# Keys and values of the third graph layer projected with seven block products in place of eight

## The chip, the cores and the metric

The kernel runs on one core of a Trainium2 chip. The metric is the device time of one execution in microseconds. A core has TensorE (PE: matmuls and transposes; PEld is its weight load), VectorE (DVE), ScalarE (ACT), GpSimd (POOL) and SyncE (SP), which run side by side, each through its own queue in order, and wait for each other through semaphores. Matmul results land in PSUM (eight banks of 512 fp32 values for each of 128 partitions), all else lies in SBUF.

## The reference, cut to what matters

Four graph layers follow each other on 2708 nodes with 512 features; each is `x = layernorm(x + gnn(x, adj))`, and the count starts at 0. The change lies in layer 2:

```python
def _L2_gnn_ref(x, adj, weight, bias, node_w, edge_w):
    node_att = jax.nn.softmax(x @ node_w, axis=0)
    h = x @ edge_w
    e = h @ h.T
    e = jnp.where(adj > 0, e, NEG_BIG)
    edge_att = jax.nn.softmax(e, axis=1)
    combined_att = node_att * edge_att
    support = x @ weight
    output = adj * combined_att @ support
    return output + bias
```

The two projections `x @ edge_w` (the keys) and `x @ weight` (the values) are 2708 x 512 by 512 x 512 products in fp32.

## The kernel before

The nodes are cut into 22 blocks of 128 rows, the last of 20 (`BLOCKS`, `NT = 22`). The 512 features are four chunks of 128 (`C = 4`). Layers 0 and 1 come first; layer 1's last sums are in `xs`, one row block after another. Layer 2 then has a stage of its own (from L1899 on) that makes, for all nodes, the transposed keys `hT` (features on partitions, nodes along), the values `sup` (nodes on partitions, by blocks), the node scores `natt`, and a copy of `x + bias` in memory (`x2_d`). The attention of layer 2 and then layer 3 follow.

In the stage, `PRE` cuts the blocks into seven groups: six of three blocks, and a last one of four (404 columns). For each group:

- `transpose_rows` (L1364) turns each block with four TensorE transposes (L1368) into one PSUM bank, and VectorE copies the bank into `xt_g` (L1369).
- `project_wide` (L1371) makes the keys: for each of four output chunks, four accumulating matmuls (L1376) whose stationary operand is a 128 x 128 piece of `edge_w` (`ew_sb`) and whose moving operand is a chunk of `xt_g`, as wide as the group; ScalarE copies each result to `hT` (L1928).
- For each block, four matmuls (L1934) with the block's piece of `xt_g` as stationary and 512 columns of `weight` (`w2_sb`) as moving operand make its values; ScalarE copies them to `sup` (L1941).
- For each block, VectorE makes the node score (`xn`, L1943) and adds the bias to `xs` (L1953), and GpSimd's queue writes that to `x2_d` (L1954).

In group 1 the layer norms of layer 1's last two blocks (L1915) come in between. After the groups the softmax over `natt` is made, with two reductions over partitions on GpSimd (L1959, L1964).

The matmuls are fp32. Each shows in the profile as two TensorE instructions of the same shape, each with its own weight load, so that 16 matmuls count as 32. A `tc.tile_pool` with `bufs=4` hands out four PSUM banks for each tag: here four for `tp` (transposes and keys) and four for `pr` (values). A bank is handed out again when the last reader of what it held is done.

The instructions of each engine are put in order when the kernel is built. So VectorE's operations for later blocks, whose inputs are ready early, can stand ahead of the copies of an earlier group: in the trace all node scores are made in the first 20 us of the stage.

The attention stage begins with `combine` (L2004): for each pair of value blocks, four VectorE operations (L2009 to L2012) on half rows, some in place in `sup`. What they write besides lies in the memory of `xs`, so the first waits until the writes to `x2_d` have landed. They stand in VectorE's queue before the last groups' values are done. SyncE's queue loads the adjacency (`a_score`, L1423), and `score_products` (L1523) multiplies keys with keys.

Of the kernel before, what the change touches and what calls it, by code (L numbers as in the profile page):

```python
# [8 lines left out]
F32 = mybir.dt.float32  # L9
# [4 lines left out]
ALU = mybir.AluOpType  # L14
# [3 lines left out]
P = 128  # L18
# [11 lines left out]
def gnn_stack_kernel(  # L30
# [83 lines left out]
    def row_stats(y, n):  # L114

        st = small.tile([P, 6], F32, tag="ln_st", name="ln_st")
        nc.vector.bn_stats(st[:n], y)
        mv = small.tile([P, 2], F32, tag="ln_mv", name="ln_mv")
        nc.vector.bn_aggr(mv[:n], st[:n])
        rstd = small.tile([P, 1], F32, tag="ln_rstd", name="ln_rstd")  # L120
        inv_std(rstd[:n], mv[:n, 1:2], LN_EPS)
        return mv[:n, 0:1], rstd[:n]

    def layer_norm(dst, y, n):
        mean, rstd = row_stats(y, n)
        nc.vector.tensor_scalar(dst, y, mean, rstd, ALU.subtract, ALU.mult)
# [62 lines left out]
    with ExitStack() as l0:  # L189
# [31 lines left out]
        def f1_tile(att, odd, name="f1b"):  # L221
            return att.tile([P, HW], F32, tag=f"f1b{odd}", name=name, bufs=HP)
# [513 lines left out]
        with (  # L736
# [4 lines left out]
            psum = first.enter_context(tc.tile_pool(name="ps_p", bufs=1, space=PSUM))  # L741
# [150 lines left out]
            def turn(k, b):  # L892
                return last_turn[0](k, b, k + 1 == HP, [])[0]
# [16 lines left out]
        with (  # L910
# [42 lines left out]
            turned = 0  # L953
            for ci, (c0, w) in enumerate(CHUNKS):
# [3 lines left out]
                for o in range(C):  # L958
# [3 lines left out]
                    ps = pair[:, o % HP, :]  # L962
                    for c in range(C):
# [15 lines left out]
                while turned < NT and sum(BLOCKS[turned]) <= c0 + w:  # L979
                    j0, n = BLOCKS[turned]  # L980
# [246 lines left out]
        xs, w1_sb, x_held = held1["xs"], held1["w1"], held1["x"]  # L1227
# [3 lines left out]
    with (  # L1231
# [12 lines left out]
        work = main.enter_context(tc.tile_pool(name="l1w", bufs=2))  # L1244
        with tc.tile_pool(name="l1a", bufs=1) as pre:
# [3 lines left out]
            turned = 0  # L1249
            for ci, (c0, w) in enumerate(PIECES):  # L1250
# [10 lines left out]
                while turned < NT and sum(BLOCKS[turned]) <= c0 + w:  # L1261
                    it = turned
                    i0, n = BLOCKS[it]
# [30 lines left out]
        for g in range(0, NT, G):  # L1294
            group = range(g, min(g + G, NT))
            c0 = g * P
            w = min(N, c0 + G * P) - c0
            if g == G:
                ew_sb = load_weight(pw2, edge_w, "ew_sb")
                w2_sb = load_weight(pw2, w2, "w2_sb")  # L1300
# [6 lines left out]
            for jt, (j0, m) in enumerate(BLOCKS):  # L1307
                if later and jt % 4 == 3:
                    y, n = later.pop(0)
                    layer_norm(y, y, n)  # L1310
                raw = work.tile([P, G * P], F32, tag="raw", name="raw", bufs=5)
                a = work.tile([P, G * P], F32R, tag="at", name="at", bufs=3)
# [9 lines left out]
                for it in group:  # L1322
                    n = BLOCKS[it][1]
                    at = a[:, (it - g) * P : (it - g) * P + n]
                    for k, half in enumerate(halves):
# [4 lines left out]
                            start=(jt == 0 and k == 0),  # L1330
                            stop=(jt == NT - 1),
                        )
            for it in group:
                n = BLOCKS[it][1]
# [24 lines left out]
    def key_tile(name):  # L1359
        t = featp.tile([P, C, NFULL * P + Q], F32, tag="keys", name=name)  # L1360
        nc.vector.memset(t[:, :, N:], 0.0)
        return t

    def transpose_rows(psum, dst, rows, n, copy):  # L1364

        tp = psum.tile([P, C, P], F32, tag="tp", name="tp")
        for c in range(C):
            nc.tensor.transpose(tp[:, c, :n], rows[:n, c * P : (c + 1) * P], ident[:n, :n])  # L1368
        copy(dst, tp[:, :, :n])  # L1369

    def project_wide(psum, w, xt, width, put):  # L1371

        for o in range(C):
            ps = psum.tile([P, BANK], F32, tag="tp", name="ps_wide")
            for c in range(C):
                nc.tensor.matmul(  # L1376
                    ps[:, :width],
                    w(c, o),
                    xt(c),
                    start=(c == 0),  # L1380
                    stop=(c == C - 1),
                )
            put(o, ps[:, :width])
# [515 lines left out]
    hT = key_tile("hT")  # L1899
    l2_values = ExitStack()  # L1900
    store = l2_values.enter_context(tc.tile_pool(name="store", bufs=1))
    sup = store.tile([P, NT, F], F32, name="sup")
    natt = const.tile([P, NT], F32, name="natt")
    nc.vector.memset(natt, -3.0e38)
    with (
        tc.tile_pool(name="l2w", bufs=2) as work,
        tc.tile_pool(name="l2ps", bufs=4, space=PSUM) as psum,
    ):
        PRE = [list(range(g, min(g + 3, NT))) for g in range(0, NT - 1, 3)]
        if NT % 3 == 1:  # L1910
            PRE[-1].append(NT - 1)
        PW = sum(BLOCKS[it][1] for it in PRE[-1])
        for gi, group in enumerate(PRE):
            for y, n in last_rows if gi == 1 else ():
                layer_norm(y, y, n)  # L1915
            c0, w = group[0] * P, sum(BLOCKS[it][1] for it in group)
            xt = work.tile([P, C, max(PW, 3 * P)], F32, tag="xt", name="xt_g")
            for b, it in enumerate(group):
                n = BLOCKS[it][1]
                transpose_rows(  # L1920
                    psum, xt[:, :, b * P : b * P + n], xs[:, it, :], n, nc.vector.tensor_copy
                )
            project_wide(
                psum,
                lambda c, o: ew_sb[:, c, o * P : (o + 1) * P],
                lambda c: xt[:, c, :w],
                w,
                lambda o, ps: nc.scalar.copy(hT[:, o, c0 : c0 + w], ps),  # L1928
            )
            for b, it in enumerate(group):  # L1930
                i0, n = BLOCKS[it]
                ps = psum.tile([P, F], F32, tag="pr", name="ps_sup")
                for c in range(C):
                    nc.tensor.matmul(  # L1934
                        ps[:n],
                        xt[:, c, b * P : b * P + n],
                        w2_sb[:, c, :],
                        start=(c == 0),
                        stop=(c == C - 1),
                    )  # L1940
                nc.scalar.copy(sup[:n, it, :], ps[:n])  # L1941
                xn = work.tile([P, F], F32, tag="xn", name="xn")
                nc.vector.scalar_tensor_tensor(  # L1943
                    xn[:n],
                    xs[:n, it, :],
                    1.0,
                    nw_sb[:n],
                    ALU.mult,
                    ALU.mult,
                    accum_out=natt[:n, it : it + 1],  # L1950
                )

                nc.vector.tensor_tensor(xs[:n, it, :], xs[:n, it, :], b2_sb[:n], ALU.add)  # L1953
                nc.gpsimd.dma_start(x2_d[i0 : i0 + n], xs[:n, it, :])  # L1954
# [21 lines left out]
    with (  # L1976
# [8 lines left out]
        held = rows_tile("held").rearrange("p t f -> p (t f)")  # L1985
# [192 lines left out]
        for t in range(start3 + steps + LAG):  # L2178
# [98 lines left out]
```

## Time and profile before

| what | value |
|---|---|
| median of three runs | 3120.9 us (3119.28 to 3121.2) |
| profiled execution, its time | 3120.7 us |
| profiled execution, its span | 3118.8 us |
| TensorE busy | 3070.6 us, 98% |
| VectorE busy | 2025.3 us, 65% |
| ScalarE busy | 1353.1 us, 43% |
| stage of the change, from its first transpose to its last L1934 pass | 1393.6 to 1553.0 us |
| L1934 (values), 176 TensorE instructions, mean | 596 ns |
| L1376 (keys), 224 TensorE instructions, mean | 489 ns |
| granted TensorE clock, mean of the execution | 0.997 |

The span runs from the first to the last instruction of the core; the time of the execution has a little around it. The duration of one instruction reaches past the start of the next, since both are pipelined: the mean of 596 ns for a 512-wide pass is more than the distance from one such pass to the next. To see what a pass takes, read the start of the first and of the one after the last, and divide by their number. In the chain of waits each piece is the time from one start to the next, so its pieces can be divided directly.

### The profile page before, as it was taken

How to read it: one execution, taken by the hardware profiler on the slowest of the kernel's cores; microseconds unless marked ns; L12 is line 12 of the kernel's file. 1: busy time of each engine (PE TensorE's matmuls, PEld its weight loads, DVE VectorE, ACT ScalarE, POOL GpSimd, SP SyncE). 2: the span in 40 equal slices, each digit the busy share in tenths (PEclk: the TensorE clock that was granted, in tenths of full speed). 3: DMA queues.
4: the chain of work that ended last, by engine and by line, in shares of the span. 5: the costliest groups of instructions: out<-in, count | busy, mean ns of one | idle time of the engine just before them, and what ended most of it. 6: DMA issues, size and time to landing. Idle time of an engine off the chain costs nothing.

```text
span 3118.8 us, 39610 instructions
## 1 busy us (share of the span) xinstructions
PE 3070.6 (98%) x15144; PEld 2336.9 (75%) x15144; DVE 2025.3 (65%) x3804; ACT 1353.1 (43%) x1655; POOL 175.2 (6%) x301
## 2 busy tenths in 40 slices
PE   8999999999999999999999999999999999999999
PEld 7999996544444447875588887787778888888886
DVE  7988966785885783452366668677555555555565
ACT  7999998587767350001133334435211111111111
POOL 1111100000000000000111101000010000000000
PEclk9999999999999999999999999999999999999999
DMA  8987964266445315530254445566331111111110
GB/s 277 333 313 251 321 235 144 79 232 221 161 173 192 108 42 158 144 97 31 67 166 133 136 138 165 164 177 184 108 95 36 50 51 51 51 51 50 50 52 29
DMA packets 207228, 430.10 MB, mean 138 GB/s; under 512 B 22218, under 2 KB 137598, under 8 KB 201294
## 3 DMA queue, kind: packets, MB, share of 16 engines
q1 hardware_dynamic: 182774, 326.20, 34.0%
q0 software_dynamic: 24256, 101.35, 8.9%
q8 instruction: 119, 1.95, 0.3%
q14 instruction: 71, 0.58, 0.1%
q10 hardware_dynamic: 8, 0.02, 0.0%
HBM read 330.07 MB, written 95.87 MB: 137 GB/s over the span
## 4 chain that ended last, share of the span: by engine, by line
PE 79%; ACT 8%; DVE 8%; issue 3%; DMA 1%; SPq 0%; DVEq 0%; ACTq 0%; POOLq 0%
PE po L1728 21%; PE ps_s L1523 18%; PE po L650 9%; PE ps_nb L1326 7%; PE ps_wide L1376 5%; PE po L548 4%; ACT t L383 4%; ACT t L515 3%; DVE t L378 2%; PE ps_v L131 2%; PE ps_sup L1934 2%; PE ps_hid L131 2%; PE ps_dec L1093 2%; PE ps_mlp L964 1%; DVE a L444 1%
## 5 line engine op out<-in xcount | busy, mean ns | idle before, releaser
L378 DVE SCALAR_TENSOR_TENSOR t<-t,a 128x2708 f32<-128x2708 f32 (+1 forms) x152 | 443.8, 2922 | 166.1 <-ACT t L383 165.8
L548 PE MATMUL po<-xw,t 128*128 128x129 f32 (+2 forms) x3872 | 428.2, 277 | 11.8 <-DVE rc L781 4.9
L548 PEld LDWEIGHTS po<-xw,t 128*128 128x128 f32 (+2 forms) x3872 | 422.8, 189 | 16.4 <-issue 7.9
L383 ACT ACTIVATE t<-f1b,f2h 128x1354 f32<-128x1354 f32 x296 | 404.4, 1412 | 34.2 <-PE po L650 34.2
L1523 PE MATMUL ps_s<-q,hT 128*128 128x256 f32 (+1 forms) x1848 | 405.5, 372 | 0.0
L1728 PE MATMUL po<-sup,e 128*128 128x256 f32 (+1 forms) x1512 | 398.2, 384 | 5.6 <-DVE c L1809 2.8
L650 PE MATMUL po<-t,emb 128*128 128x452 f32 (+3 forms) x1056 | 399.1, 547 | 4.3 <-ACT t L635 4.2
L1523 PEld LDWEIGHTS ps_s<-q,hT 128*128 128x128 f32 x1848 | 339.5, 190 | 49.5 <-issue 5.1
L650 PEld LDWEIGHTS po<-t,emb 128*128 128x128 f32 (+1 forms) x1056 | 194.2, 191 | 202.1 <-issue 189.2
L1728 PEld LDWEIGHTS po<-sup,e 128*128 128x128 f32 (+1 forms) x1512 | 264.7, 185 | 59.6 <-issue 19.8
L1728 PE MATMUL po<-held,T 128*128 128x256 f32 x1200 | 293.8, 380 | 0.0
L1728 PEld LDWEIGHTS po<-held,T 128*128 128x128 f32 x1200 | 227.0, 190 | 31.1 <-issue 0.9
L2129 DVE SCALAR_TENSOR_TENSOR e<-a_cols,ps_s 128x512 f32<-128x512 f32 (+1 forms) x121 | 79.6, 658 | 233.8 <-PE ps_s L1523 229.9
L1523 PE MATMUL ps_s<-hT 128*128 128x256 f32 (+2 forms) x968 | 213.8, 372 | 0.8 <-ACT sup L1941 0.7
L515 ACT ACTIVATE t<-t 128x2708 f32<-128x2708 f32 x88 | 209.2, 2377 | 8.8 <-DVE t L378 8.1
L1523 PEld LDWEIGHTS ps_s<-hT 128*128 128x128 f32 x968 | 175.1, 190 | 29.1 <-issue 3.9
L1326 PE MATMUL ps_nb<-hid_hi,at 128*128 128x512 f32 x484 | 185.6, 390 | 0.4 <-DVE at L1318 0.4
L635 ACT ACTIVATE t<-t 128x2708 f32<-128x2708 f32 x64 | 157.3, 2458 | 60.4 <-DVE t L378 60.2
L1326 PE MATMUL ps_nb<-hid_lo,at 128*128 128x512 f32 x462 | 180.0, 390 | 0.0
L2031 ACT ACTIVATE a_score<-a_score,neg_big 128x512 f32<-128x512 f32 (+3 forms) x131 | 88.4, 683 | 196.0 <-DMA a_score<-in_adjT_dram 98.9
L2121 ACT ACTIVATE q<-ps_wide,uq 128x256 f32<-128x256 f32 (+1 forms) x44 | 20.5, 465 | 335.7 <-PE ps_wide L1376 335.7
L1633 ACT ACTIVATE e<-e 128x512 f32<-128x512 f32 (+1 forms) x187 | 113.8, 615 | 118.2 <-DVE e L1632 117.9
(276 smaller groups left out, 3995.4 us busy)
## 6 DMA issues: line engine op xcount, KB each, us to landing
a<-adj_d SPq DMA_DIRECT2D x113, 677.0 KB
a_cols<-in_adjT_dram SPq DMA_DIRECT2D x200, 256.0 KB
kept<-t POOLq DMA_DIRECT2D x20, 1354.0 KB, 8.4
t<-kept SPq DMA_DIRECT2D x20, 1354.0 KB
raw<-in_adjT_dram SPq DMA_DIRECT2D x105, 256.0 KB
a<-in_adjT_dram SPq DMA_DIRECT2D x37, 677.0 KB
adj_d<-a POOLq DMA_DIRECT2D x37, 677.0 KB, 6.2
a_score<-in_adjT_dram SPq DMA_DIRECT2D x55, 256.0 KB
```

The lines of the kernel that those rows point to most:

```text
L131: nc.tensor.matmul(ps[:n], xt[:, c, :n], w[:, c, :], start=(c == 0), stop=(c == C - 1))
L378: return nc.vector.scalar_tensor_tensor(t, t, GUARD, ab, ALU.add, ALU.mult)
L383: done = nc.scalar.activation(t[:, k, :], f1b[k][:n, :w], AF.Tanh, bias=f2h[:n, jt, h : h + 1], scale=0.5,)
L515: nc.scalar.activation(t, t, AF.Exp, scale=0.5)
L548: nc.tensor.matmul(po[k][b][:m, s * DR : (s + 1) * DR], t[own : own + n, k, i0 : i0 + m], values[own : own + n, jt, HP * p + k, :], start= ...
L635: nc.scalar.activation(t, t, AF.Exp, scale=0.5)
L650: nc.tensor.matmul(po[HB * k + q][:, :qw], values[r : r + n, jt, h * P : (h + 1) * P], t[r : r + n, k, q0 : q0 + qw], start=(place == 0), ...
L1326: nc.tensor.matmul(pos[it][:n], at, half[:, jt, :], start=(jt == 0 and k == 0), stop=(jt == NT - 1),)
L1376: nc.tensor.matmul(ps[:, :width], w(c, o), xt(c), start=(c == 0), stop=(c == C - 1),)
L1523: nc.tensor.matmul(ps[:, jb, i:w], keys[:, c, j : j + P], st["q"][:, c, i:], start=(c == 0), stop=(c == C - 1),)
L1633: return nc.scalar.activation(e, e, AF.Exp)
L1728: nc.tensor.matmul(po[bank][rows, half, :], lhsT, rhs, start=(k == 0 and half == 0) if first is None else first, stop=last, skip_group_che ...
```

## The change

Blocks 0 to 19 form five groups of four (`QUADS`); blocks 20 and 21 are a last group that is projected as before. For a group of four, x (512 rows by 512 features) and each weight matrix are cut in halves both ways, into four quarters of 256 x 256. Rows are halved by the parity of the block (`i`), features into the first and last two chunks (`j`). Each projection is then made of seven products of quarters or sums of quarters in place of eight products of quarters (the form of Strassen's scheme with fifteen additions):

- `weight_sums`: four sums of quarters for each weight matrix, made once, on VectorE. Two of the eight lie in `sup`'s rows of blocks 20 and 21, which are filled last.
- `turn`: transposes a group (the copies to `xt_g` are ScalarE's now) and makes four sums of its quarters (`s_g`), which serve keys and values. Group 0 is turned ahead of the loop, and each group's successor ahead of its own products.
- `seven`: seven products, each in one bank of the ring `pr` (four banks); the first is copied out by ScalarE, and seven VectorE additions for each projection, each with one operand in PSUM, form the four quarters of the result in `hT` or `sup`.
- `edge_product` and `value_product`: the four matmuls of one product, each 256 columns wide.

The node scores and the bias follow in a loop of their own after a group's products, as before one for each block; `xn` has one buffer in place of two. The sums have six tiles more and `xt_g` is 512 columns wide.

```diff
-        PRE = [list(range(g, min(g + 3, NT))) for g in range(0, NT - 1, 3)]
...
+        QUADS = [list(range(g, g + 4)) for g in range(0, NT - 3, 4)]
+        PRE = QUADS + [list(range(4 * len(QUADS), NT))]
...
+        def weight_sums(w, held):
+
+            b11, b12, b21, b22 = (quarter(w, j, l) for j in range(2) for l in range(2))
+            t1, t2, t3, t4 = (t.rearrange("p (j f) -> p j f", j=2) for t in held)
+            tt(t1, b12, b11, ALU.subtract)
+            tt(t2, b22, t1, ALU.subtract)
+            tt(t3, b22, b12, ALU.subtract)
+            tt(t4, b21, t2, ALU.subtract)
+            return b11, b21, t2, t3, t4, t1, b22
+
+        def turn(gi):
...
+                transpose_rows(
+                    psum, xt[:, :, b * P : b * P + n], xs[:, it, :], n, nc.scalar.copy
+                )
...
+            a = xt.rearrange("p (j c) (g i n) -> p j c g i n", j=2, g=2, i=2)
+            a11, a12, a21, a22 = (a[:, j, :, :, i, :] for i in range(2) for j in range(2))
+            s = work.tile([P, 4, 2, 2, P], F32, tag="s", name="s_g")
+            s1, s2, s3, s4 = (s[:, k] for k in range(4))
+            tt(s1, a21, a22, ALU.add)
+            tt(s2, s1, a11, ALU.subtract)
+            tt(s3, a11, a21, ALU.subtract)
+            tt(s4, a12, s2, ALU.subtract)
+            turned[-1] = xt, (a11, a12, s2, s3, a22, s1, s4)
+
+        def seven(lefts, rights, product, out):
...
+            nc.scalar.copy(m1, made(0))
+            dst = out(0, 0)
+            tt(dst, like(made(1), dst), like(m1, dst), ALU.add)
+            tt(u2, made(2), m1, ALU.add)
+            tt(u3, made(3), u2, ALU.add)
+            dst = out(1, 0)
+            tt(dst, like(made(4), dst), like(u3, dst), ALU.add)
+            ps = made(5)
+            dst = out(1, 1)
+            tt(dst, like(ps, dst), like(u3, dst), ALU.add)
+            tt(u2, ps, u2, ALU.add)
+            dst = out(0, 1)
+            tt(dst, like(made(6), dst), like(u2, dst), ALU.add)
+
+        def edge_product(ps, left, right):
+            for o in range(2):
+                for c in range(2):
+                    nc.tensor.matmul(
+                        ps[:, o * 2 * P : (o + 1) * 2 * P].rearrange("p (g n) -> p g n", g=2),
+                        right[:, c, o * P : (o + 1) * P],
+                        left[:, c],
+                        start=(c == 0),
+                        stop=(c == 1),
+                    )
+
+        def value_product(ps, left, right):
+            for g in range(2):
+                for c in range(2):
+                    nc.tensor.matmul(
+                        ps[:, g * HALF : (g + 1) * HALF],
+                        left[:, c, g, :],
+                        right[:, c, :],
+                        start=(c == 0),
+                        stop=(c == 1),
+                    )
+
+        held = work.tile([P, 6, F], F32, tag="held", name="held_sums", bufs=1)
+        held = [held[:, k] for k in range(6)] + [sup[:, it, :] for it in PRE[-1]]
+        ew_sums, w2_sums = weight_sums(ew_sb, held[:4]), weight_sums(w2_sb, held[4:])
+        turn(0)
         for gi, group in enumerate(PRE):
...
+            if gi + 1 < len(PRE):
+                turn(gi + 1)
...
+            if lefts:
...
+                seven(lefts, ew_sums, edge_product, lambda i, l: keys[:, l, :, :, i, :])
...
+                seven(lefts, w2_sums, value_product, lambda i, l: rows[:, :, i, l, :])
+            else:
...
```

More of the change, by code (lines that the diff above doesn't have):

```diff
@@ L1908, in gnn_stack_kernel, with quarter @@
     ):
-        PRE = [list(range(g, min(g + 3, NT))) for g in range(0, NT - 1, 3)]
-        if NT % 3 == 1:
-            PRE[-1].append(NT - 1)
-        PW = sum(BLOCKS[it][1] for it in PRE[-1])
+        QUADS = [list(range(g, g + 4)) for g in range(0, NT - 3, 4)]
+        PRE = QUADS + [list(range(4 * len(QUADS), NT))]
+        assert all(BLOCKS[it][1] == P for group in QUADS for it in group)
+        HALF = F // 2
+        tt = nc.vector.tensor_tensor
+        turned = []
+        def quarter(w, j, l):
+            return w[:, 2 * j : 2 * j + 2, l * HALF : (l + 1) * HALF]
@@ new lines, in weight_sums @@
+        def weight_sums(w, held):
[7 more added lines that the diff above has]
+        def turn(gi):
+            group = PRE[gi]
+            xt = work.tile([P, C, 4 * P], F32, tag="xt", name="xt_g")
+            for b, it in enumerate(group):
+                n = BLOCKS[it][1]
+                transpose_rows(
+                    psum, xt[:, :, b * P : b * P + n], xs[:, it, :], n, nc.scalar.copy
+                )
+            turned.append((xt, ()))
+            if len(group) < 4:
+                return
+            a = xt.rearrange("p (j c) (g i n) -> p j c g i n", j=2, g=2, i=2)
[7 more added lines that the diff above has]
+            turned[-1] = xt, (a11, a12, s2, s3, a22, s1, s4)
@@ new lines, in seven, with made, like @@
+        def seven(lefts, rights, product, out):
+            m1, u2, u3 = (
+                work.tile([P, BANK], F32, tag=f"sum{k}", name=f"sum{k}", bufs=1)
+                for k in range(3)
+            )
+            def made(k):
+                ps = psum.tile([P, BANK], F32, tag="pr", name="ps_seven")
+                product(ps, lefts[k], rights[k])
+                return ps
+            def like(x, dst):
+                if len(dst.shape) == 3:
+                    return x.rearrange("p (a b) -> p a b", a=dst.shape[1])
+                return x.rearrange("p (a b c) -> p a b c", a=dst.shape[1], b=dst.shape[2])
+            nc.scalar.copy(m1, made(0))
[11 more added lines that the diff above has]
+            tt(dst, like(made(6), dst), like(u2, dst), ALU.add)
@@ new lines, in edge_product @@
+        def edge_product(ps, left, right):
[17 more added lines that the diff above has]
+                        stop=(c == 1),
+                    )
@@ L1915, in gnn_stack_kernel @@
                 layer_norm(y, y, n)
+            if gi + 1 < len(PRE):
+                turn(gi + 1)
             c0, w = group[0] * P, sum(BLOCKS[it][1] for it in group)
-            xt = work.tile([P, C, max(PW, 3 * P)], F32, tag="xt", name="xt_g")
-            for b, it in enumerate(group):
-                n = BLOCKS[it][1]
[L1920 to L1931, printed above, removed]
+            xt, lefts = turned[gi]
+            if lefts:
+                keys = hT[:, :, c0 : c0 + w].rearrange(
+                    "p (l o) (g i n) -> p l o g i n", l=2, g=2, i=2
+                )
+                seven(lefts, ew_sums, edge_product, lambda i, l: keys[:, l, :, :, i, :])
+                rows = sup[:, group[0] : group[0] + 4, :].rearrange(
+                    "p (g i) (l f) -> p g i l f", i=2, l=2
+                )
+                seven(lefts, w2_sums, value_product, lambda i, l: rows[:, :, i, l, :])
+            else:
+                project_wide(
+                    psum,
+                    lambda c, o: ew_sb[:, c, o * P : (o + 1) * P],
+                    lambda c: xt[:, c, :w],
+                    w,
+                    lambda o, ps: nc.scalar.copy(hT[:, o, c0 : c0 + w], ps),
+                )
+            for b, it in enumerate(group) if not lefts else ():
+                n = BLOCKS[it][1]
                 ps = psum.tile([P, F], F32, tag="pr", name="ps_sup")
@@ L1941, in gnn_stack_kernel @@
                 nc.scalar.copy(sup[:n, it, :], ps[:n])
-                xn = work.tile([P, F], F32, tag="xn", name="xn")
+            for it in group:
+                i0, n = BLOCKS[it]
+                xn = work.tile([P, F], F32, tag="xn", name="xn", bufs=1)
                 nc.vector.scalar_tensor_tensor(
```

## The prediction

> **What bounds the kernel now.** I read the page first (busy rows, chain of waits by line), then the chain in order of time around layer 2's projections, the busy windows of that stretch, and the timelines of TensorE and VectorE for the duration of each kind of instruction.
>
> ```profile
> span 3118.8 us, 39610 instructions
> PE 3070.6 (98%) x15144; PEld 2336.9 (75%) x15144; DVE 2025.3 (65%) x3804; ACT 1353.1 (43%) x1655; POOL 175.2 (6%) x301
> ```
>
> TensorE is busy 98% of the span, so an average hides little here. The stretch that the change rewrites, in the chain of waits in order of time:
>
> ```profile
> 1393.59 1.52 PE tp L1368 x12
> 1395.10 1.90 PE ps_sup L1934 x4
> 1397.00 10.32 PE ps_wide L1376 x32
> 1407.32 8.58 PE ps_sup L1934 x20
> ...
> 1530.01 10.85 PE ps_wide L1376 x32
> 1540.87 12.14 PE ps_sup L1934 x28
> 1553.01 0.02 issue
> 1553.02 2.78 DMA a_score<-in_adjT_dram
> ```
>
> ```profile
> core 0: us, PE busy (x) PEld busy (x) DVE busy (x) ACT busy (x) POOL busy (x), PEclk, DMA share, GB/s
> 1393.60:1553.00 159.40, 159.39 (x488) 84.51 (x488) 57.25 (x143) 27.84 (x54) 12.89 (x24) 1.00 0.12 43
> ```
>
> From 1393.6 to 1553.0 us TensorE never stops, at a granted clock of 1.00, while VectorE works 57 of 159 us and ScalarE 28. So in this stage a TensorE microsecond removed is a microsecond gained, until VectorE, which gets the new additions, fills up. Durations of one instruction overlap, so I use pitches, start to start. An fp32 matmul is two instructions (two passes, each with its own weight load).
>
> ```profile
> 1632.55 3.62 PE L1523 MATMUL ps_s<-hT 128*128 128x256 f32 x16
> 1636.00 1.46 PE L1728 MATMUL po<-sup,e 128*128 128x256 f32 x6
> ...
> 3014.89 4.27 PE L1376 MATMUL ps_wide<-hT,mqk 128*128 128x148 f32 x32
> 3019.00 2.18 PE L1523 MATMUL ps_s<-q,hT 128*128 128x148 f32 x16
> ```
>
> A pass 256 wide: (1636.00 - 1632.55)/16 = 0.216 us. 148 wide: 4.11/32 = 0.128 us. From the chain: 512 wide 12.14/28 = 0.434 us, 384 wide 10.32/32 = 0.3225 us, a transpose about 0.11 us. The weight loads (190 ns each) lie hidden under all of these.
>
> **The change, part by part: TensorE.** Before, the stretch is 72.8 us for keys (six groups of 10.32, one of 10.85), 76.9 for values (six of 1.90 + 8.58 = 10.48, and 1.91 + 12.14 = 14.05) and 9.7 for transposes: 159.4. After, blocks 0 to 19 form five groups of four; each projection of a group is seven products of four matmuls, 8 passes 256 wide: 5 x 2 x 7 x 8 = 560 passes x 0.216 = 121.0 us. Blocks 20 and 21 stay as they were: 32 passes 148 wide, 4.1 us, and 16 passes 512 wide, 6.9 us. The transposes are the same 88 instructions, 9.7 us. Sum 141.7, so 17.7 us less. (The expected eighth of 20 blocks' 136 us is 17.0; the narrow last key group, 4.1 us against the 404-wide 10.85, is in both sums.)
>
> **VectorE and ScalarE.** Removed from VectorE: 22 transposed-block copies, which ScalarE takes. Added to VectorE: 8 sums of weights once, 4 sums of x per group (20), 7 additions per projection and group (70). ScalarE loses 28 + 22 evacuations but for 4 + 2, and gains 22 copies and 10 first-product copies. It has 28 us of work in 159 before and less after, so these cost nothing. For VectorE:
>
> ```profile
> 1602.12 0.68 DVE L1495 TENSOR_TENSOR mx<-e 128x512 f32<-128x512 f32 x1
> 1602.72 0.28 DVE L1684 TENSOR_TENSOR T<-e,T 128x128 f32<-128x128 f32 x1
> 1602.92 0.68 DVE L2028 SCALAR_TENSOR_TENSOR e<-a_score,ps_s 128x512 f32<-128x512 f32 x1
> 1603.52 0.68 DVE L1674 TENSOR_TENSOR acc<-acc,e 128x512 f32<-128x512 f32 x1
> ```
>
> A 128x512 operation on two tensors has a pitch of 0.60 us, also with one from PSUM (1602.92 to 1603.52). I take 0.605; the upper end is 0.715, the pitch of the two PSUM-reading L1336 at 1392.12 (1.40 us for two, each some 0.69 to 0.71).
>
> [...]
>
> In the order as built, VectorE first does the 8 weight sums and the 8 sums of x for groups 0 and 1, then additions mixed with all of the xn products (L1943) and the +b2 adds, which are pulled forward. The first two groups are thus the tight place. Check one: product 2 of group 0 needs the sum s2. VectorE reaches its end after 8 + 3 operations: 1393.6 + 11 x 0.605 + 0.1 = 1400.3 us. TensorE gets there after 32 transposes (3.5 us; two groups are turned first) and two products (3.46): 1400.5. So between 0 and 1 us of wait (0.9 at a pitch of 0.70); I take 0.3. Check two: four PSUM banks hold the products, so product k waits for the reader of product k-4. The tightest is product 5 of group 1's keys, which TensorE reaches at 1393.6 + 3.5 + 24.2 + 1.75 + 5 x 1.73 = 1431.7, while the addition that frees its bank has ahead of it, itself included, 53 full operations and 3.0 us of small ones (last rows' layer norm): 53 x 0.605 + 3.0 = 35.1, so 1428.7. Three us to spare; the limit is a pitch of 0.66. Later groups have 22 operations, 13.3 us, under 26 of TensorE.
>
> **Waits and moved work.** The first of layer 2's in-place value combinations (L2009) waits for the last x2_d writes, 3.3 us before:
>
> ```profile
> 1534.65 0.42 DVE L2009 TENSOR_TENSOR held<-sup 128x256 f32<-128x256 f32 x1 [3.30 <-DMA x_d<-xs]
> ```
>
> It now stands in VectorE's queue inside the last group's key additions, with the addition of product 2 behind it. TensorE can make products 2 to 5 meanwhile, 6.9 us, so 3.3 are covered; without that cover the cost is 3.3. The 41 combinations (pitch 0.335, 13.7 us) and 14 additions (8.5) fit in the last group's 24 us and the 11 us of the last pair behind it. The 22 x2_d writes stay on POOL's queue, spread over more time; the +b2 adds that feed them end sooner than before. The natt maximum and sum cross POOL behind 12 writes in place of 3, with two POOL waits of about 1 us on VectorE in group 1, inside its slack. SP's queue has the same loads in the same order; the first for attention (a_score, 1553.02) start when the last L1934 pass has read the released memory, and so move with it. No order outside this stage differs.
>
> **Sum.** 159.4 - 141.7 = 17.7 gained, 0.3 lost: 17.4 us. Profiled span 3118.8 - 17.4 = 3101.4, its run 3120.7 - 17.4 = 3103.3; the median of the runs is 3120.9, 0.2 above that run, so 3103.5.
>
> **Rivals.** (1) VectorE becomes the bound in groups 0 and 1. At a pitch of 0.70, near L1336's, check one costs 0.9 and check two 53 x 0.70 + 3.0 = 40.1 against the 38.1 + 0.9 that TensorE has, 1.1; the remaining 30 operations of group 1 add 0.1 each, 3.0, as there is no slack left to take them. Together 5.0 in place of 0.3: 3108.2. Speaking for it: 83 operations in 53 us. Against: the pitch of L2028, L1495 and L1674.
>
> (2) A pass costs more than 0.216, because bank, weights and operand change after every second pass. The group's row says 405.5/1848 = 0.219, and eight passes at 1620.12 end at 1621.94, 0.2275 each. 560 x 0.0115 = 6.4 less: 3109.9. Against: L1523 also loads new weights for each pass.
>
> (3) The other side, slower than before: keys products 0, 1 and 4 stream x through a view of two runs of 128 columns with a gap. 3 x 8 x 5 = 120 passes; no row before streams such a view. The lower end is two passes of 128, as in the transposes, 2 x 0.11, no more than now; the upper end is half rate, 0.216 more for each, 25.9 us: 3129.4. It decides from 0.145 more per pass (17.4/120). I take the lower end, as a 128-wide row costs only its width. [...]
>
> **Chances.** Forecast 0.77 (3102 to 3106), rival 1 0.13, rival 2 0.05, rival 3 0.05. A measurement of this kernel tells changes from about 0.2%, 6.2 us; the first three cases lie beyond that. Faster 0.93, same 0.02, slower 0.05. The range takes in rival 1 and leaves out 2 and 3: 3101.5 to 3109.
>
> **What would show it.** Right: the stretch from the first transpose to the last ps_sup pass takes about 142 us; ps_seven passes have a pitch of 0.216 and TensorE shows at most 1 us of idle time there; the chain stays on TensorE. Rival 1 shows as TensorE idle released by VectorE between 1395 and 1450, rival 2 as a wider pitch in all ps_seven passes, rival 3 as a wider pitch in three of seven key products alone. The forecast is wrong if VectorE's additions from PSUM run above 0.66 us apart, or if the stretch after 1553 loses what this one gains.

## The result, and the profile after

The changed kernel takes 3102.8 us, the median of six runs (3100.5 to 3104.0), against 3119.1 for the kernel before, also the median of six. The ratio is 0.9947, with an interval of 0.9936 to 0.9958: between 13.1 and 20.0 us faster. The forecast was 3103.5, from a stage that gets 17.4 us shorter.

The first lines of the changed kernel's page: TensorE has the same 98%, with 208 more instructions (104 matmuls, most of them narrower) in 17.7 us less.

```profile
span 3101.1 us, 40133 instructions
...
PE 3052.9 (98%) x15352; PEld 2376.3 (77%) x15352; DVE 2073.6 (67%) x3880; ACT 1345.9 (43%) x1643; POOL 175.3 (6%) x301
```

The chain of waits in order of time through the rewritten stage of the changed kernel (start, duration, what):

```profile
1392.99 3.70 PE tp L1368 x32
1396.70 12.09 PE ps_seven L1985 x56
1408.79 12.09 PE ps_seven L1996 x56
...
1498.64 0.79 PE tp L1368 x8
1499.43 12.28 PE ps_seven L1985 x56
1511.71 12.09 PE ps_seven L1996 x56
1523.80 4.03 PE ps_wide L1376 x32
1527.83 6.99 PE ps_sup L2036 x16
1534.81 0.02 issue
```

All of it is TensorE's work, laid end to end. L1985 makes the keys' products and L1996 the values'; each seven products take 12.09 us for 56 passes, 0.2159 us each; only the keys of the last group of four, behind the transposes of the 20-row block, take 12.28. The last pair follows with 4.03 us for keys and 6.99 for values. From the first transpose to the end of the last ps_sup pass the stage takes 1534.81 - 1392.99 = 141.8 us, where it took 1553.01 - 1393.59 = 159.4 before: 17.6 less.

The busy windows of the changed kernel, one row for each group of four and a last one for blocks 20 and 21 (the window, its length, then the busy time of each engine with its instructions, the granted clock, and the DMA share):

```profile
core 0: us, PE busy (x) PEld busy (x) DVE busy (x) ACT busy (x) POOL busy (x), PEclk, DMA share, GB/s
1392.98:1420.90 27.92, 27.92 (x146) 25.03 (x147) 27.92 (x61) 5.59 (x12) 3.28 (x6) 1.00 0.15 56
1420.90:1446.80 25.90, 25.90 (x130) 23.00 (x129) 24.53 (x58) 4.91 (x9) 4.00 (x8) 1.00 0.17 63
1446.80:1472.70 25.90, 25.90 (x130) 23.00 (x129) 14.31 (x23) 3.23 (x6) 2.34 (x4) 1.00 0.11 41
1472.70:1498.60 25.90, 25.90 (x131) 23.00 (x129) 14.30 (x22) 3.23 (x6) 2.17 (x4) 1.00 0.11 41
1498.60:1523.80 25.20, 25.20 (x123) 22.16 (x122) 20.75 (x48) 1.88 (x4) 1.11 (x2) 1.00 0.20 65
1523.80:1534.80 11.00, 11.00 (x48) 5.92 (x47) 3.98 (x10) 1.72 (x5) 0.00 (x0) 1.00 0.01 1
sum 141.82, PE 141.82 PEld 122.11 DVE 105.78 ACT 20.55 POOL 12.89; mean PE 23.64 PEld 20.35 DVE 17.63 ACT 3.43 POOL 2.15
```

The third column is TensorE: it equals the length of its window in every row, so nothing waits. The fifth is VectorE, which before was busy for 57 of 159 us and now for 106 of 142. In the first group it never rests (27.92 of 27.92) and in the second hardly (24.53 of 25.90): that is the tight place that the prediction named. It is still not the bound, because nothing that TensorE needs next is late.

The span falls by 17.7 us. The stage gives 17.6 of it; it starts 0.6 us earlier, and what follows it takes 0.5 longer (1566.3 against 1565.8). In the profiles of the experiments below, whose code ahead of the stage is the same, the stage starts anywhere between 1390.1 and 1394.6 us. That scatter moves a run by some 2 us either way, while the stage's own length repeats: 141.82 us here, 141.8 in a second profile of the same kernel. The experiments are therefore read by the length of the stage first, and by the runs' times second.

### The profile page after: what moved, and what is told of

Same layout as the page of the kernel before. It is cut to its first block, busy times and chain, and to the rows that moved or that the text cites. A ratio compares the mean times of both kernels' runs of the same rounds, so it can differ in the third digit from the quotient of the medians.

```text
span 3101.1 us, 40133 instructions
## 1 busy us (share of the span) xinstructions
PE 3052.9 (98%) x15352; PEld 2376.3 (77%) x15352; DVE 2073.6 (67%) x3880; ACT 1345.9 (43%) x1643; POOL 175.3 (6%) x301
## 4 chain that ended last, share of the span: by engine, by line
PE 79%; ACT 8%; DVE 8%; issue 3%; DMA 1%; POOL 0%; SPq 0%; DVEq 0%; ACTq 0%; POOLq 0%
PE po L1728 21%; PE ps_s L1523 19%; PE po L650 10%; PE ps_nb L1326 7%; ACT t L383 4%; PE po L548 4%; ACT t L515 3%; PE ps_wide L1376 3%; PE ps_hid L131 2%; PE ps_v L131 2%; DVE t L378 2%; PE ps_seven L1985 2%; PE ps_seven L1996 2%; PE ps_dec L1093 2%; PE ps_mlp L964 1%
## 5 line engine op out<-in xcount | busy, mean ns | idle before, releaser
L1523 PE MATMUL ps_s<-q,hT 128*128 128x256 f32 (+1 forms) x1848 | 405.6, 372 | 0.0
L1523 PEld LDWEIGHTS ps_s<-q,hT 128*128 128x128 f32 x1848 | 339.9, 190 | 49.0 <-issue 4.9
L1523 PE MATMUL ps_s<-hT 128*128 128x256 f32 (+2 forms) x968 | 213.8, 372 | 0.7 <-ACT sup L2043 0.7
L1523 PEld LDWEIGHTS ps_s<-hT 128*128 128x128 f32 x968 | 175.4, 191 | 28.7 <-issue 3.9
```

What stands on the lines that cost most here:

```text
L1523: nc.tensor.matmul(ps[:, jb, i:w], keys[:, c, j : j + P], st["q"][:, c, i:], start=(c == 0), stop=(c == C - 1),)
```

## The experiments

The theory: the gain is TensorE's passes alone, seven products in place of eight in two projections; all that was added lies under TensorE's work. The rivals: the gain, or a part, comes from the new grouping; VectorE, or the ring of banks, or ScalarE's copies limit the stage already or nearly. Each kernel below starts from the changed kernel and computes the reference's result.

### Eight products in the same groups

The groups of four, ScalarE's copies and the order of the loops stay; the scheme itself goes.

```diff
             turned.append((xt, ()))
-            if len(group) < 4:
-                return
+            return
...
-        held = work.tile([P, 6, F], F32, tag="held", name="held_sums", bufs=1)
-        held = [held[:, k] for k in range(6)] + [sup[:, it, :] for it in PRE[-1]]
-        ew_sums, w2_sums = weight_sums(ew_sb, held[:4]), weight_sums(w2_sb, held[4:])
```

> Groups of four, turned ahead, copies on ScalarE, as in the changed kernel, but eight products in place of seven (the old matmuls: keys 512 wide, values 512 wide) and no sums. Theory (the gain is the eighth product): 5 x 32 passes for keys x 0.434 = 69.4 us, 4.1 for the last pair, 176 passes for values 76.4, transposes 9.8: the stage from first transpose to last ps_sup pass takes 159.7 us, as long as before (159.4), and the time is within 0.1% of before, about 3120. Rival (the gain comes from regrouping, turning ahead and moving the copies): the stage is near 142 us and the time near 3103. If both share, between.

Measured: 3118.2 us, median of ten runs, against 3119.2 for the kernel before; ratio 0.9996 (0.9987 to 1.0005), no change. From the chain of waits of this kernel:

```profile
1394.57 13.73 PE ps_wide L1376 x32
1408.31 13.73 PE ps_sup L2032 x32
...
1542.16 6.99 PE ps_sup L2032 x16
```

The stage runs from 1390.87 to 1549.15: 158.3 us. The grouping gives 1.1 us of stage (a 512-wide value pass has 13.73/32 = 0.429 us here, where the groups of three had 10.48/24 = 0.437), too little to tell in the runs. The other 158.3 - 141.8 = 16.5 us belong to the seven products.

### Keys alone, values alone

In the first the values are made as before, block by block; in the second the keys are, by `project_wide`. The four weight sums that are then not needed go too.

```diff
-                seven(lefts, w2_sums, value_product, lambda i, l: rows[:, :, i, l, :])
...
-            for b, it in enumerate(group) if not lefts else ():
+            for b, it in enumerate(group):
```

> Seven products for the keys, eight for the values of all blocks. Theory (price per pass, the same for both forms): 280 passes x 0.216 = 60.5, last keys 4.0, 176 passes x 0.434 = 76.4, transposes 9.8: stage 150.7 us, 8.9 more than the changed kernel, time about 3111.7. Rival (the keys' products, whose moving operand is a view with gaps, cost more and give less than half): stage above 152 us here.

```diff
-                seven(lefts, ew_sums, edge_product, lambda i, l: keys[:, l, :, :, i, :])
+                project_wide(
+                    psum,
+                    lambda c, o: ew_sb[:, c, o * P : (o + 1) * P],
+                    lambda c: xt[:, c, :w],
+                    w,
+                    lambda o, ps: nc.scalar.copy(hT[:, o, c0 : c0 + w], ps),
+                )
```

> Eight products for the keys (512 wide), seven for the values. Theory: 69.4 + 4.0 + 60.5 + 7.0 + 9.8 = 150.7 us for the stage, the same as with the keys alone, time about 3111.7. Rival (the values carry the gain): stage below 148 us here and above 152 with the keys alone.

Measured: keys alone 3112.8 us, ratio 0.9976 (0.9965 to 0.9987); values alone 3112.8, ratio 0.9978 (0.9968 to 0.9988). The first group in the chains, keys alone and then values alone:

```profile
1393.80 12.09 PE ps_seven L1985 x56
1405.88 13.73 PE ps_sup L2035 x32
```

```profile
1396.64 13.74 PE ps_wide L1376 x32
1410.38 12.09 PE ps_seven L1996 x56
```

Whichever projection uses seven products takes 12.09 us a group, and the other 13.73. Both stages last 150.05 us (1390.10 to 1540.15, and 1392.94 to 1542.99), halfway between 158.3 and 141.8: 8.2 us for each projection, which is five groups of 13.73 - 12.09 = 1.64. The two gains add without a remainder, so neither half is paid for by the other. A whole eighth would be 1.72 a group; the narrower pass (0.2159 against half of 0.429, 0.2145) takes the missing 0.08.

### The copies of the transposed blocks back on VectorE

```diff
-                    psum, xt[:, :, b * P : b * P + n], xs[:, it, :], n, nc.scalar.copy
+                    psum, xt[:, :, b * P : b * P + n], xs[:, it, :], n, nc.vector.tensor_copy
```

> The changed kernel with the 22 copies of transposed blocks back on VectorE. In the order as built VectorE does the 8 weight sums first and then the copies of group 0, so the transposes' four banks stay full: the fifth block's transposes wait until about 0.1 + 8 x 0.60 + 0.6 us after the start where TensorE is there after 1.75, 3.8 us, and then go at VectorE's pitch, 0.5 more. Theory (VectorE's queue is what could hold TensorE up, at the start above all): stage 146 us, 4.3 more than the changed kernel, all of it TensorE idle in the first 8 us, none later; time about 3107. Rival (VectorE is full in groups 0 and 1, so 12 more operations there cost their 7 us): idle also between 1400 and 1450, stage about 150 us. Rival (no effect, as VectorE has slack): stage 142 us.

Measured: 3107.4 us, ratio 0.9965 (0.9952 to 0.9978); stage 1393.80 to 1540.65, 146.85 us, 5.0 more than the changed kernel. TensorE's timeline at its start:

```profile
1393.80 1.97 PE L1368 MATMUL tp<-ident,xs 128*128 128x128 f32 x16 [1.26 <-DVE hT L1361]
1399.22 3.30 PE L1368 MATMUL tp<-ident,xs 128*128 128x128 f32 x16 [3.46 <-DVE xt_g L1369]
```

The whole loss is here. The second group's transposes wait 3.46 us until VectorE copies a block of the first group out of its PSUM bank, which it does only behind the eight weight sums, and then run at VectorE's pace, 3.30 us where group by group they take 1.75: 3.46 + 1.55 = 5.0. No other idle time appears in the stage, although VectorE has the same first two groups to get through with 12 more operations. Moving the copies to ScalarE, costed at nothing in the prediction, is what makes the start free; ScalarE is busy for 20.6 of 142 us.

### More additions

How far is VectorE from being the bound? Six of the seven additions of each projection are made twice, and in a second kernel three times (the repeats write the same values again).

```diff
-            tt(u2, made(2), m1, ALU.add)
+            ps = made(2)
+            tt(u2, ps, m1, ALU.add)
+            tt(u2, ps, m1, ALU.add)
```

> Six of the seven additions of each projection are made twice, with the same result: 60 more VectorE operations of 0.60 us in the stage, 36 us, on top of 105.8 busy in 141.8. Theory (VectorE is only filled up; the order as built moves the node scores and bias adds out of the way, and four banks bridge the rest): TensorE stays without idle, stage 142 us, VectorE busy to the brim (about 140) and done some 1 us after TensorE; time within 2 us of the changed kernel. Rival (groups 0 and 1, where VectorE is already busy all the time, take the 24 operations on the path): stage 150 us or more, time about 3113.

> The same six additions made three times: 120 more VectorE operations, 72 us, 178 us of VectorE work in all. Theory (beyond the brim VectorE is the bound and every further operation costs its 0.60 us): stage 178 us, 36 more than the changed kernel, TensorE idle in nearly all groups, released by the additions; time about 3139, slower than the kernel with eight products. Rival (TensorE still sets the time): stage under 150 us.

Measured with 60 more: 3101.9 us, two runs, ratio 0.9936 (0.9916 to 0.9956). Its stage, as one window:

```profile
1390.74:1532.56 141.82, 141.80 (x696) 121.85 (x696) 138.44 (x278) 20.48 (x42) 12.95 (x24) 1.00 0.14 49
```

The stage is as long as before to the hundredth. VectorE is busy for 138 of its 142 us, and its 33 additional microseconds cost nothing.

With 120 more: 3128.2 us, median of eight, ratio 1.0023 (1.0013 to 1.0033), slower than the kernel before. Of this kernel one window and the sum of six that span 1393.86 to 1562:

```profile
1420.00:1450.00 30.00, 24.49 (x118) 20.25 (x117) 30.00 (x60) 3.63 (x8) 2.16 (x4) 1.00 0.10 36
...
sum 168.14, PE 150.43 PEld 121.43 DVE 166.41 ACT 21.12 POOL 14.36; mean PE 25.07 PEld 20.24 DVE 27.74 ACT 3.52 POOL 2.39
```

Now VectorE fills nearly the whole of each window, and TensorE rests for 5.5 us of the 30 shown. What ended these waits stands in the groups by line, here of products 0 and 1 of the values (behind the second bar the idle time before their passes, in total):

```profile
L2013 PE MATMUL ps_seven<-w_sb,xt_g 128*128 128x256 f32 x80 | 19.7, 389 | 8.0 <-DVE sum L1981 5.0 <-ACT sum L1968 3.0
```

L1981 is the last repeat of the addition that makes `u3`, on VectorE, and L1968 is ScalarE's copy of a first product. This is the picture that rival 1 would have given. The stage lasts 165.4 us (1393.86 to 1559.25), not the expected 178, and VectorE is busy for 163.7 of them. The 41 value combinations, 13.7 us of VectorE's work, were counted into the stage, and were built behind the additions, so that 31 of them, 10.4 us, ran after it (from 1559 to 1574, during the attention); what made the other 2.2 us is not shown. Read together, the two kernels put the limit between 138 and 164 us of VectorE's work, which fits the point where that work reaches TensorE's 142 us. The changed kernel has 106.

### A ring of two banks

```diff
-                ps = psum.tile([P, BANK], F32, tag="pr", name="ps_seven")
+                ps = psum.tile([P, BANK], F32, tag="pr", name="ps_seven", bufs=2)
...
-                ps = psum.tile([P, F], F32, tag="pr", name="ps_sup")
+                ps = psum.tile([P, F], F32, tag="pr", name="ps_sup", bufs=2)
```

> The ring of product banks has two banks in place of four (transposes keep their four). Theory (an addition follows its product by about 0.24 + 0.7 us, less than the 1.73 of the next product, so two banks do except where VectorE is late): TensorE idles about 1.7 us at the start, where product 3 waits for the addition of product 1 behind the 16 sums, and 1 to 2 us in the last group, where that addition stands behind value combinations; stage about 145 us, time about 3106. Rival (each product waits for its predecessor's reader): 70 x 0.5 us or more, stage above 170. Rival (no effect): 142.

Measured: 3103.3 us, two runs, ratio 0.994 (0.9921 to 0.996); stage 1391.23 to 1534.07, 142.84 us, 1.0 more than with four banks where 3 were expected. TensorE's timeline of this kernel, near the start and in the last group:

```profile
1399.95 1.36 PE L1368 MATMUL tp<-ident,xs 128*128 128x128 f32 x11
...
1510.73 2.61 PE L1996 MATMUL ps_seven<-w_sb,xt_g 128*128 128x256 f32 x11 [0.24 <-DVE sum L1978]
```

The products do wait for their banks early on, but the order as built puts eleven of a later group's transposes into that gap, so that little is idle; TensorE works 142.44 of the 142.84 us. In the last group, where the value combinations stand between VectorE's additions, the seven key products take 12.52 us (1498.21 to 1510.73), 0.24 of it the wait in the last row. Two banks would nearly do here; the four are cover that the order as built barely uses.

### A better version?

The last block has 20 rows, and its 8 value passes cost as much as a full block's, about 3.5 us (half of the last pair's 6.99). This candidate makes them as four products in four 32-row strips of one bank, side by side, and adds the strips with one matmul by stacked identities (`quarters`).

```diff
+                    nc.tensor.matmul(
+                        parts[c * Q : (c + 1) * Q],
+                        xt[:, c, P : P + Q],
+                        w2_sb[:, c, :],
+                        start=True,
+                        stop=True,
+                    )
...
+                nc.tensor.matmul(ps[:REST], quarters[:, :REST], few, start=True, stop=True)
```

> A candidate that adds to the changed kernel: the values of the last block (20 rows) are made by four products of 32 rows side by side in the array, one for each chunk of features, and one matmul that sums the four parts, in place of 8 passes 512 wide. The row of such side-by-side products (L1542) takes 0.57 us for 8 passes 256 wide. So 8 x 0.14 + 2 x 0.43 = 2.0 us in place of 3.5: stage 1.4 us shorter, 140.4; in the time, 0.05%, not to be told from the changed kernel. Rival (passes of 512 columns don't run side by side): stage 142.7 us, 0.9 longer.

Measured: 3105.8 us, median of four, ratio 0.9947 (0.993 to 0.9963). The stage is 1.4 us shorter, as expected (1393.78 to 1534.19, 140.4), and the time is none the shorter, though at 0.05% it could not have shown in the runs. TensorE's timeline and then ScalarE's:

```profile
1528.53 1.06 PE L2037 MATMUL ps_few<-w_sb,xt_g 128*32 128x512 f32 x8
1529.53 3.70 PE L2050 MATMUL ps_sup<-w_sb,xt_g 128*128 128x512 f32 x8
...
1540.71 0.33 PE L1555 MATMUL ps_s<-ident,s_own 128*128 128x128 f32 x1 [2.10 <-ACT s_own L1537]
```

```profile
1539.79 0.72 ACT L2153 ACTIVATE a_score<-a_score,neg_big 128x512 f32<-128x512 f32 x1 [2.27 <-DMA a_score<-in_adjT_dram]
```

Behind the stage TensorE stands idle for 2.1 us, before the first matmul that reads `s_own`. That tile is a copy on ScalarE, which stands behind an `a_score` row that waits for its load. The load is of the adjacency, which starts only when the stage's last wide values pass has released its memory: in the chain of waits that pass ends at 1533.24, and SyncE issues the first load at 1533.26. To settle whether this belongs to the candidate or to one run, both kernels ran again on one chip, the changed kernel as it is:

> The changed kernel itself, on the same chip as the candidate beside it. Stage 141.8 us again; no TensorE idle of more than 0.3 us at the first own-block transpose of attention (L1555).

> The candidate for the 20-row block a second time. In its first run the stage was 140.4 us, but TensorE then idled 2.1 us at L1555, behind the third a_score load. Theory A (the loads can only start when the last wide ps_sup pass has read x, so a shorter end leaves their landing uncovered): the idle comes again, about 1 to 2 us, and the time equals the changed kernel's. Theory B (that landing was late by chance): idle under 0.5 us and the span 1 us shorter from the stage's start on. The times of both differ by less than can be told.

Measured: the changed kernel 3102.5 us (3100.9 to 3104.6), ratio 0.9945 (0.9931 to 0.9958); the candidate 3104.4 (3104.2 to 3105.3), ratio 0.9952 (0.994 to 0.9965). ScalarE's timeline of the changed kernel, then of the candidate:

```profile
1539.39 1.34 ACT L2135 ACTIVATE a_score<-a_score,neg_big 128x512 f32<-128x512 f32 x2 [2.41 <-DMA a_score<-in_adjT_dram]
1540.63 0.25 ACT L1537 COPY s_own<-ps_s 128x128 f32<-128x128 f32 x1
1543.02 0.72 ACT L2135 ACTIVATE a_score<-a_score,neg_big 128x512 f32<-128x512 f32 x1 [2.15 <-DMA a_score<-in_adjT_dram]
```

```profile
1535.40 1.37 ACT L2153 ACTIVATE a_score<-a_score,neg_big 128x512 f32<-128x512 f32 x2 [1.47 <-DMA a_score<-in_adjT_dram]
1538.40 0.72 ACT L2153 ACTIVATE a_score<-a_score,neg_big 128x512 f32<-128x512 f32 x1 [1.63 <-DMA a_score<-in_adjT_dram]
1539.03 0.24 ACT L1537 COPY s_own<-ps_s 128x128 f32<-128x128 f32 x1
```

In the changed kernel the `s_own` copy stands between the second and the third `a_score` row; in the candidate the third row stands ahead of it, waits 1.63 us for its load, and TensorE loses 1.59 us at the same matmul. So in both profiles of the candidate the 1.4 us were lost again within 7 us of the stage's end. The load itself comes no later in the candidate: the third row starts 6.0 and 6.5 us after the first load is issued there, and 5.6 and 6.6 us in the two profiles of the changed kernel. What differs is its place in ScalarE's queue. No version here beats the changed kernel. Whether the candidate would win with `s_own` kept ahead of the third row wasn't tried.

## Why the prediction was right

**What bounds the kernel.** "A TensorE microsecond removed is a microsecond gained" held for the change: the stage got shorter by 17.6 us and the span by 17.7. Within the stage it held as well for the keys alone, for the values alone, with 60 more additions and for the candidate. Behind the stage it did not hold for the candidate, whose 1.4 us were lost again.

**The passes.** The 560 passes have the forecast pitch, 0.2159 against 0.216, but for the 0.19 us that the last group's keys took more; the kernel with eight products has the same excess there (13.93 against 13.73), so it isn't the scheme's. The last pair took 4.03 and 6.99 us against 4.1 and 6.9, the transposes 9.7 as forecast; 141.8 in all against 141.7. Keys-alone and values-alone show that the two halves are equal and additive. Of the 17.6 us, the kernel with eight products gives 16.5 to the seven products and 1.1 to the groups of four, a division that the sum didn't make. With the pitch falls rival 2, a dearer pass: 0.2275 would have made 12.74 us of each 12.09.

**Rival 3, the view of two runs with a gap.** TensorE's timeline of the changed kernel in the first group's keys (the last row is product 5 of the second group's, for check two below); products 0, 1 and 4 stream such views of `xt_g`, the rest contiguous sums from `s_g`:

```profile
1396.53 3.62 PE L1985 MATMUL ps_seven<-xt_g,ew_sb 128*128 128x256 f32 x16
1399.99 3.62 PE L1985 MATMUL ps_seven<-s_g,held_sums 128*128 128x256 f32 x16
1403.44 1.89 PE L1985 MATMUL ps_seven<-xt_g,held_sums 128*128 128x256 f32 x8
1405.17 1.89 PE L1985 MATMUL ps_seven<-s_g,held_sums 128*128 128x256 f32 x8
1406.89 1.89 PE L1985 MATMUL ps_seven<-s_g,ew_sb 128*128 128x256 f32 x8
...
1431.09 1.89 PE L1985 MATMUL ps_seven<-s_g,held_sums 128*128 128x256 f32 x8
```

Sixteen passes take 3.46 us from start to start with the gap (1396.53 to 1399.99) and 3.45 without (to 1403.44); eight take 1.73 with it and 1.72 without (1403.44, 1405.17, 1406.89). The gap costs nothing that shows, 0.216 us a pass for both. The products' outputs in PSUM are without a gap here, so these rows tell of the moving operand alone, which is read from SBUF.

**Check one and check two, and rival 1.** VectorE's timeline of the changed kernel (the second column is the duration, and the pitch is from start to start):

```profile
1398.89 0.67 DVE L1946 TENSOR_TENSOR s_g<-s_g,xt_g 128x512 f32<-128x512 f32 x1
1399.49 0.67 DVE L1945 TENSOR_TENSOR s_g<-xt_g 128x512 f32<-128x512 f32 x1
...
1402.50 0.67 DVE L1970 TENSOR_TENSOR hT<-ps_seven,sum 128x512 f32<-128x512 f32 x1
1403.10 0.67 DVE L1971 TENSOR_TENSOR sum<-ps_seven,sum 128x512 f32<-128x512 f32 x1
1403.70 0.67 DVE L2047 SCALAR_TENSOR_TENSOR xn<-xs,nw_sb 128x512 f32<-128x512 f32 x1
...
1426.79 0.68 DVE L1970 TENSOR_TENSOR hT<-ps_seven,sum 128x512 f32<-128x512 f32 x1
...
1503.19 0.69 DVE L1970 TENSOR_TENSOR hT<-ps_seven,sum 128x512 f32<-128x512 f32 x1 [2.63 <-PE ps_seven L1985]
```

Check one: s2 is ready at 1399.56 and TensorE comes for it at 1399.99, the next row of its timeline above; 0.43 us to spare. The working gave 0.2 (1400.3 and 1400.5), and the 0.3 us of wait was taken out of a range of 0 to 1 all the same; it did not come. Check two: the addition that frees product 5's bank ends at 1427.5 and TensorE reaches that product at 1431.09 (forecast 1428.7 and 1431.7, from a start 0.6 later): 3.6 us to spare, where 3 were forecast. Rival 1 needed a pitch above 0.66; the additions from PSUM have 0.60 (1402.50 to 1403.10 to 1403.70), the same as a sum from SBUF (1398.89 to 1399.49). The upper end of 0.715 was a misreading: the two L1336 operations last 0.73 to 0.75 us each and 1.40 together, so that the second starts 0.65 to 0.67 after the first; they also read a third operand, which the additions don't. An operand in PSUM beside one in SBUF adds nothing that shows. The check of the 53 operations was right, but the tight place is softer than it looks: with 60 more additions, some 24 of them in the first two groups, TensorE still never waits, because the order as built then holds other work back: the changed kernel has 22 of the node scores' products (L2047) in the first two groups, that one 8.

**The wait for x2_d.** Before, the first in-place combination (L2009, now L2113) waited 3.3 us. In the changed kernel's groups by line, over the stage (busy, mean, and behind the second bar the idle time before them):

```profile
L2113 DVE TENSOR_TENSOR held<-sup 128x256 f32<-128x256 f32 x10 | 4.2, 416 | 0.1
```

Of 3.3 us, 0.1 is left. The stores still leave late, the last two at 1500.26 on POOL's queue, but VectorE now has a wait of its own ahead of the combination: it stood idle for 2.63 us until TensorE had made product 1 (L1970, at 1503.19, the last row of its timeline above), and the stores land meanwhile, 2.7 and 2.3 us after their issue. So the cost of 0 was right, but not for the reason given: the ring's 6.9 us of cover was not needed.

**The stage behind.** The first adjacency loads start at 1534.83, as the last pass ends (1534.81), and moved with it as forecast; TensorE has no idle time at the first matmul that reads `s_own`. That this was not to be taken for granted is shown by the candidate, whose shorter stage lost its gain just there. In the changed kernel the order there is the one of before, as the prediction said ("No order outside this stage differs"): the `s_own` copy stands between the second and the third `a_score` row.

**The sum.** 17.6 us of stage against 17.4, and 3102.8 against 3103.5. The one term of the sum that was off is the 0.3 us wait for s2, which measured 0. That the median agrees to 0.7 us is in part luck: the forecast took 17.4 us off 3120.9, the median of three runs of the kernel before; over six runs it is 3119.1, and the medians differ by 16.3. The stage's length, which repeats, is the firmer agreement. The moved copies were put at nothing because ScalarE has room; that was right, but the sum doesn't show that the same copies on VectorE would have cost 5.0 us.

## What to carry to other kernels

Where one engine is busy without a gap and at full clock, cost a change by that engine's pitch for the new shape, and then check, operation by operation, only the few moments at which another engine's result is due; here the stage's sum came out within 0.2 us, and the time to spare at the two checks within 0.6. Work moved to a neighbour engine was free here until it filled the stage (106 us of work in 142 cost nothing, 138 nothing, and 164 went with a stage 24 us longer), but at the start of the stage the copies of the first two groups, on the busy engine, already cost 5 us. A gain at a stage's end was lost again here, where what was queued next waited for a load that the stage's end releases (the candidate's 1.4 us, to waits of 2.10 and 1.59 us): look at the first engine that copies for the bottleneck there.

## What the runs showed of the hardware that was not expected

- A moving operand in two runs of 128 columns with a gap streams as fast as a contiguous one: 0.216 us a pass, 256 wide.
- Eight 512-wide fp32 passes into four 32-row strips of one bank took 1.00 us together (1528.53 to 1529.53 in the candidate, where the next pass starts), against half of 6.99 us for eight passes of 20 rows in one strip: the strips run side by side at 512 columns too, as L1542's did before at 256 (in the chain of waits 0.57 us for eight passes from 1622.01, where the eight L1523 passes ahead of them, as wide, took 1.73).
- A 128x512 addition on VectorE with one operand in PSUM is followed by the next after 0.60 us, as from SBUF.
- Weight loads of 190 ns (the mean at L1985 and L1996) under passes of 216 ns hold TensorE up nowhere in the stage, though weight loads fill 122 of its 142 us in all.
